# Moving residuals and block sums to GpSimd, the per-row constant to ScalarE, and reordering VectorE's first work in a two-layer graph kernel

## The chip, the core and the metric

The kernel runs on one core of a Trainium2 chip, in one launch. The metric is the device time of that launch in microseconds (us): a median of 1521.02 us over three runs, which lie between 1520.96 and 1525.21 us. One more execution was recorded by the hardware profiler. It took 1521.21 us, and the span from its first to its last instruction was 1519.2 us. All times with decimals below are from that execution, counted from the start of its span.

Five engines work side by side, each on a queue of its own: TensorE (PE in the profile; its weight loads are the row PEld), VectorE (DVE), ScalarE (ACT), GpSimd (POOL) and SyncE (SP, which here only issues DMAs).

## What is computed

The input x has 128 batches b, each of 128 rows (nodes) and 512 columns. The matrix adj is 128x128 and sparse. Cut to what matters:

```python
h = relu(layernorm(x))                        # over the 512 columns
A = einsum('od,bdn->bon', adj, h); C = A + b0 # layer 0: both weights are adj
x = x + max_over_last(relu(A[:, :, None, :] + (C - A)[:, :, :, None]))
h = relu(layernorm(x))                        # layer 1
q, k, v = h @ Wq + bq, h @ Wk + bk, h @ Wv + bv
w = softmax(q @ k.T / 8 + (adj == 0) * -1e9)  # 8 heads of 64
x = x + w @ v
```

Since C - A is the bias b0 of the row, layer 0 adds one number per row and batch, c = relu(max of A over the columns + b0). A constant added to a row doesn't change its layernorm, so both layers use the same h. The output is thus x + c + attention(h), and the bias of v can be added to x.

## The kernel before

**Groups.** Four batches make a group; there are 32 groups, g = 0 to 31, with b = 4g the first batch of group g and m = b + 8 the first batch of the group two further on. The kernel is software-pipelined over groups: while group g is attended to, q and k of group g+1 are computed, and the norms of group g+2.

**Products.** The projections h·W are 512x512 by 512x(4·128), done with seven block products in place of eight (p1, p6, p2, p7, p5, p4, p3), on sums and differences of the blocks of W and of h. p4 and p3 of most groups are split once more in the same way into 128x128 blocks (p43a and p43b). These need:
- sums of W: `weight_sums` (L381) and, one level down, `weight_blocks` (L369), made once per weight;
- sums of h: `h_sum` (L345, four per group) and, one level down, `h_blocks` (L354 to L356, two calls of three instructions per group), which fill the tile h2, of which there is one buffer.

TensorE multiplies (`mm` L418, `block_mm` L484); VectorE and ScalarE take results out of PSUM (L433, L439, L457, L466, L487). In `p43b`, TensorE writes a scratch bank, VectorE adds it to the tile u (L487, in `more`), and TensorE's last four matmuls of p43b write the same scratch bank again.

**Norms.** `norm(m)` makes statistics on VectorE (L279 to L282) and, on GpSimd, the reciprocal deviation and its product with the mean (L284, L286). `norm_end(m)` applies them on ScalarE (L289) and then adds the bias of v to x on GpSimd (L295, `add_bv`). `blocks(m)` transposes h in 32x32 blocks on VectorE (L302) and `move` sends two batches of them with 16 DMAs on SP's queue to their places in the tile hT (L312). `adjacency(m)` multiplies h by adj on TensorE (L327) and takes the maximum on VectorE (L328); every fourth one makes c (L330).

**Attention.** `scores` (L567, exponentials on ScalarE L575), `mask` (L579, eight per group, on GpSimd except at the end), `apply` (L597; VectorE divides by the sums, L614 and L615), and `residual` (L625): out = x + c + o in one VectorE instruction per batch, followed by the DMA to out (L629). In the last group, two of the four go to ScalarE and GpSimd (L627, L628).

**The order is written out by hand.** Within `tc.manual_schedule()` each engine executes its instructions in the order in which the program emits them. A group is `apply` of the group before, `scores`, and then 18 steps (six in the last group, which has v alone), most of them one product; a table `todo` says what is emitted after the product of each step:

```python
part += [[p.p1], [p.p6], [p.p2]]                       # v, then q and k of g+1
...
    part += [[p.p7, p.p43a], [p.p5], [p.p43b]]         # steps 3, 4, 5 for v
...
for s, ps_ in enumerate(part):
    for p in ps_:
        p()
    for f, *args in todo[s]:
        f(*args)
```

So work given to step 4 stands, on its engine, behind what p5 of v emits and ahead of what p43b of v emits. Group 0, the last but one (group 30) and the last one have tables that differ in places. The beginning, ahead of the loop, is a straight list (L655 to L697): norms of group 0, transposes and q of group 0 by plain products (`plain_q`), sums of Wk and of h, norms of group 1, and then the seven products of k of group 0.

Of the kernel before, what the change touches and what calls it, by code (L numbers as in the profile page):

```python
# [47 lines left out]
AF = mybir.ActivationFunctionType  # L48
ALU = mybir.AluOpType
# [4 lines left out]
G = 4  # L54
# [113 lines left out]
def tile_adj_preln_d2(  # L168
# [13 lines left out]
    nc = tc.nc  # L182
    B, D, N = x.shape
    NG = B // G
# [22 lines left out]
    def fast(ctx):  # L207
# [8 lines left out]
        CNT, w_of, O = [], {}, {}  # L216
        X, HN, TB, HT, HB, H2, QT, KT, C, AMAX, WA, RSTD, NMR, PR = ({} for _ in range(14))
# [5 lines left out]
        def x_of(b):  # L223
            return X[b // 2][:, b % 2, :]
# [63 lines left out]
        def norm_end(m):  # L288
            nc.scalar.activation(HN[m], x_of(m), AF.Relu, scale=RSTD[m], bias=NMR[m])  # L289
            if m >= G:  # L290
                add_bv(m)
# [32 lines left out]
        def adjacency(m):  # L324
            g, i = divmod(m, G)
            pa = bank(7 if g > 0 else 5 + i % 2)
            nc.tensor.matmul(pa, adjT, HN[m], start=True, stop=True)  # L327
            nc.vector.reduce_max(AMAX[g][:, i : i + 1], pa, axis=AX.X)  # L328
            if i == G - 1:
                nc.vector.tensor_scalar(C[g], AMAX[g], b0_sb, 0.0, op0=ALU.add, op1=ALU.max)  # L330
# [9 lines left out]
        def h_sum(g, k):  # L340

            o, a, b = ("t1 b12 b11", "t2 b22 t1", "t3 b22 b12", "t4 b21 t2")[k].split()
            if k == 0:
                h_quarters(g)
            nc.vector.tensor_sub(HB[g][o], HB[g][a], HB[g][b])  # L345

        def h_blocks(g, k):

            if k == 0:
                H2[g] = one.tile([P, 2, 4, D], F32, name="h2")  # L350
            b = HB[g]["b22 t4".split()[k]].rearrange("p t c d -> p c t d")
            t = H2[g][:, 1 - k]

            nc.vector.tensor_sub(t[:, 0:2], b[:, :, 1], b[:, 0])  # L354
            nc.vector.tensor_sub(t[:, 2], b[:, 1, 1], t[:, 0])
            nc.vector.tensor_sub(t[:, 3], b[:, 1, 0], t[:, 2])  # L356

        def weight_blocks(eng, n):

# [29 lines left out]
        class Products:  # L389
# [48 lines left out]
            def add(self, out, bank, more):  # L438
                nc.vector.tensor_tensor(out, self.view(bank), self.view(more), op=ALU.add)  # L439
# [141 lines left out]
        def apply(g, n_last=G):  # L581
# [31 lines left out]
            for po, rs, oo in parts:  # L613
# [3 lines left out]
                    rs.unsqueeze(2).to_broadcast([P, rs.shape[1], HD]), op=ALU.mult,  # L617
                )

        def residual(b, eng=nc.vector):  # L620
            g, i = divmod(b, G)
            y = O[g][:, i]
            x_b, c_b = x_of(b), C[g][:, i : i + 1]
            if eng is nc.vector:
                eng.scalar_tensor_tensor(y, x_b, c_b, y, op0=ALU.add, op1=ALU.add)  # L625
            else:
                nc.scalar.activation(x_b, x_b, AF.Identity, bias=c_b)  # L627
                eng.tensor_tensor(y, x_b, y, op=ALU.add)  # L628
            nc.sync.dma_start(out[b], y)  # L629

        def count(b0, b1):
# [10 lines left out]
        def next_norms(m):  # L642

            return {
                0: [(norm_end, m), (norm, m + 1), (norm_end, m + 1)],
                7: [(adjacency, m)], 8: [(norm, m + 2), (norm_end, m + 2), (blocks, m)],
                9: [(blocks, m + 1), (move, m + 1)],
                12: [(norm, m + 3), (norm_end, m + 3), (adjacency, m + 1)],
                13: [(blocks, m + 2)],
                14: [(blocks, m + 3), (move, m + 3), (adjacency, m + 2)],  # L650
            }

        with tc.manual_schedule():

            for m in range(G):  # L655
                norm(m)
                if m < 2:
                    norm_end(m)
            transposes(0)
            transposes(1)  # L660
            norm_end(2)
            norm_end(3)
            nc.vector.tensor_single_scalar(live, adjT, 0.0, op=ALU.not_equal)
            adjacency(0)
            adjacency(1)
            transposes(2)
            transposes(3)
            weight_sums(nc.gpsimd, "v")
            plain_q(0, 0)
            adjacency(2)  # L670
            plain_q(0, 1)
            adjacency(3)
            weight_sums(nc.vector, "k")
            for k in range(4):
                h_sum(0, k)
            norm(G)
            norm_end(G)
            norm(G + 1)
            norm_end(G + 1)
            plain_q(1, 0)  # L680
            blocks(G)
            blocks(G + 1)
            move(G + 1)
            plain_q(1, 1)
            k = Products(0, "k")
            more = {
                0: [(adjacency, G), (norm, G + 2), (norm_end, G + 2)],
                1: [(norm, G + 3), (norm_end, G + 3), (blocks, G + 2)],
                2: [(adjacency, G + 1)], 3: [(blocks, G + 3), (move, G + 3)],
                4: [(adjacency, G + 2)], 5: [(adjacency, G + 3)],  # L690
            }
            for s, p in enumerate((k.p1, k.p6, k.p2, k.p7, k.p5, k.p4, k.p3)):
                p()
                for f, m in more.get(s, ()):
                    f(m)
            weight_sums(nc.gpsimd, "q")
            weight_blocks(nc.gpsimd, "q")  # L697
            for g in range(NG):
                b = g * G
                if g > 0:  # L700
                    apply(g - 1)
                scores(g)
                part = []
                for p in [Products(g, "v")] + [Products(g + 1, n) for n in "qk" if g + 1 < NG]:
                    part += [[p.p1], [p.p6], [p.p2]]
                    if p.n == "v" and g in (0, NG - 1):
                        part += [[p.p7], [p.p5], [p.p4, p.p3]]
                    else:
                        part += [[p.p7, p.p43a], [p.p5], [p.p43b]]
                todo = {s: [] for s in range(len(part))}  # L710

                def add(s, *what):
                    todo[s].append(what)

                m = b + 2 * G
                if g + 1 < NG:
                    if g > 0:
                        for i in range(G):
                            residual(b - G + i)
                    if m < B:  # L720
                        norm(m)
                    if 0 < g < NG - 1:
                        add(0, adjacency, m - 1)
                    for k, s in enumerate((1, 2, 2, 3) if g > 0 else (3, 3, 4, 5)):
                        add(s, h_sum, g + 1, k)
                    for k, s in enumerate((6, 7)):
                        add(s, h_blocks, g + 1, k)
                    if g + 2 < NG:
                        for s, l in next_norms(m).items():
                            for what in l:  # L730
                                add(s, *what)
                    else:
                        add(6, count, 0, b)
                    eng = nc.gpsimd if m < B else nc.vector
                    at = (8, 9, 9, 10, 10, 13, 14, 15) if m < B else (4, 8, 8, 12, 12, 13, 14, 14)
                    for k, s in enumerate(at):
                        add(s, mask, eng, b + k // 2, k % 2)
                    if g + 2 < NG:
                        add(0, load, 2 * g + 5)
                    if g + 3 < NG:  # L740
                        add(8, load, 2 * g + 6)
                else:
                    for k, s in enumerate((0, 0, 0, 0, 2, 2, 3, 4)):
                        add(s, mask, nc.vector, b + k // 2, k % 2)
                    for i, s in enumerate((0, 0, 0, 1)):
                        add(s, residual, b - G + i)
                if g == 0:
                    add(8, weight_blocks, nc.gpsimd, "k")
                    for i in range(G):
                        add(15, add_bv, i)  # L750
                    add(15, weight_blocks, nc.gpsimd, "v")
# [6 lines that stand above are left out]
            g = NG - 1  # L758
            apply(g, 2)
            count(B - 2 * G, B)  # L760
            for i in range(G):
                residual(g * G + i, nc.gpsimd if i < 2 else nc.vector)
            pc = bank(1)
            for k in range(2):
                nc.tensor.matmul(pc[0:1, 0:1], CNT[k], ones, start=k == 0, stop=k == 1)
            nc.scalar.copy(flag, pc[0:1, 0:1])
# [38 lines left out]
```

## Time and profile before

| | busy us | share of the span |
|---|---|---|
| TensorE matmuls (PE) | 1499.8 | 99% |
| TensorE weight loads (PEld) | 1323.4 | 87% |
| VectorE (DVE) | 1152.1 | 76% |
| GpSimd (POOL) | 597.3 | 39% |
| ScalarE (ACT) | 426.6 | 28% |

A matmul's row starts when the one ahead of it has been let go, not when it has ended: they are pipelined, so a row's length is more than its share of the engine. What a matmul costs TensorE is read from one start to the next. In the timeline a row "1.89 PE ... x8" is eight matmuls; the next row starts 1.73 us after it where nothing waits, 0.216 us for each. Likewise the 128x128 block products start 0.112 us apart, and an adjacency product (two instructions) takes 0.86 us. Groups 1 to 29 start 46.57 us after one another. The granted clock of TensorE is full in all stretches up to 1480 us.

### The profile page before, as it was taken

The numbers are of one execution on the slowest core, as the hardware profiler recorded it, in microseconds if no ns is written. First come the engines' busy times: TensorE is split into PE (matmuls) and PEld (weight loads), VectorE is DVE, ScalarE is ACT, GpSimd is POOL, SyncE is SP. The second block draws the span as 40 slices with busy tenths as digits, with TensorE's granted clock in tenths as the row PEclk, the third lists the DMA queues.
The fourth block names the chain that finished last, engine by engine and source line by source line (L and its number), as shares of the span: only waits on it lengthen the run. The fifth ranks groups of instructions, "written<-read, shape, count | busy, mean of one in ns | idle before, by whom it ended". The sixth has DMA issues, their size and how long they took to land.

```text
span 1519.2 us, 32776 instructions
## 1 busy us (share of the span) xinstructions
PE 1499.8 (99%) x12909; PEld 1323.4 (87%) x12909; DVE 1152.1 (76%) x2485; ACT 426.6 (28%) x844; POOL 597.3 (39%) x670
## 2 busy tenths in 40 slices
PE   7999999999999999999999999999999999999997
PEld 5888888888888888898888888888988888888887
DVE  5577777777787777777777877777777778777776
ACT  3223232222232232323322332323233222222221
POOL 4574443343432444423434324344234343243400
PEclk9999999999999999999999999999999999999999
DMA  4233122332222321223312223222233122232211
GB/s 165 54 83 84 27 74 73 81 84 47 58 74 75 84 70 40 74 73 82 85 29 75 73 77 84 59 49 74 73 84 84 28 74 73 78 84 41 53 35 57
DMA packets 307803, 105.28 MB, mean 69 GB/s; under 512 B 273152, under 2 KB 273280, under 8 KB 307648
## 3 DMA queue, kind: packets, MB, share of 16 engines
q1 hardware_dynamic: 307328, 102.84, 26.1%
q8 instruction: 103, 1.69, 0.5%
q14 instruction: 52, 0.43, 0.1%
q0 software_dynamic: 176, 0.27, 0.1%
q10 hardware_dynamic: 144, 0.07, 0.0%
HBM read 37.03 MB, written 33.55 MB: 46 GB/s over the span
## 4 chain that ended last, share of the span: by engine, by line
PE 96%; DVE 2%; POOL 1%; ACT 0%; issue 0%; DMA 0%; DVEq 0%; POOLq 0%; ACTq 0%
PE bk L418 54%; PE bk L484 19%; PE bk L597 8%; PE bk L567 8%; PE bk L327 7%; PE bk L543 0%; POOL w L579 0%; POOL ssk_sb L369 0%; PE bk L321 0%; DMA xp<-in_x_dram 0%; POOL rstd L284 0%; DVE sk_sb L381 0%; POOL xp L295 0%; DVE hs L345 0%; ACT hn L289 0%
## 5 line engine op out<-in xcount | busy, mean ns | idle before, releaser
L284 POOL TENSOR_TENSOR rstd<-ve,mhalf 128x1 f32<-128x1 f32 x128 | 71.0, 554 | 703.9 <-DVE ve L282 703.6
L487 DVE TENSOR_TENSOR u<-u,bk 128x256 f32<-128x256 f32 x552 | 206.4, 415 | 127.5 <-PE bk L484 123.2
L579 POOL TENSOR_TENSOR w<-w,live 128x512 f32<-128x512 f32 x240 | 297.6, 1274 | 0.0
L575 ACT ACTIVATE w<-bk 128x512 f32<-128x512 f32 x256 | 128.8, 625 | 363.5 <-PE bk L567 363.5
L295 POOL TENSOR_TENSOR xp<-xp,bv_sb 128x512 f32<-128x512 f32 x128 | 165.8, 1297 | 117.9 <-ACT hn L289 117.9
L418 PEld LDWEIGHTS bk<-hs,sk_sb 128*128 128x128 f32 x768 | 143.6, 190 | 44.7 <-issue 29.2
L418 PE MATMUL bk<-hs,sk_sb 128*128 128x256 f32 x768 | 181.3, 379 | 0.0
L418 PE MATMUL bk<-sv_sb,hs 128*128 128x256 f32 x768 | 181.2, 379 | 0.0
L418 PE MATMUL bk<-hs,sq_sb 128*128 128x256 f32 x744 | 175.9, 379 | 0.1
L418 PEld LDWEIGHTS bk<-sv_sb,hs 128*128 128x128 f32 x768 | 143.6, 190 | 31.1 <-issue 14.3
L418 PEld LDWEIGHTS bk<-hs,sq_sb 128*128 128x128 f32 x744 | 138.9, 190 | 18.1 <-DVE u L457 0.5
L289 ACT ACTIVATE hn<-xp,nmr,rstd 128x512 f32<-128x512 f32 x124 | 100.9, 814 | 169.1 <-POOL nmr L286 169.0
L328 DVE TENSOR_REDUCE amax<-bk 128x1 f32<-128x512 f32 x128 | 87.9, 686 | 56.4 <-PE bk L327 56.4
L327 PE MATMUL bk<-hn,adjT 128*128 128x512 f32 x248 | 126.7, 592 | 0.3 <-ACT hn L289 0.3
L597 PE MATMUL bk<-v,w 128*64 128x65 f32 x4096 | 126.5, 222 | 0.0
L597 PEld LDWEIGHTS bk<-v,w 128*64 128x64 f32 x4096 | 122.1, 137 | 4.1 <-issue 0.3
L418 PE MATMUL bk<-hT,wk_sb 128*128 128x256 f32 x512 | 121.2, 380 | 3.1 <-ACT u L433 3.1
L418 PE MATMUL bk<-wv_sb,hT 128*128 128x256 f32 x512 | 124.3, 386 | 0.0
L567 PE MATMUL bk<-qT,kT 64*128 64x128 f32 x2048 | 122.9, 275 | 0.0
L567 PEld LDWEIGHTS bk<-qT,kT 64*128 64x128 f32 x2048 | 116.8, 188 | 2.5 <-issue 0.3
L418 PE MATMUL bk<-hT,wq_sb 128*128 128x256 f32 x496 | 117.3, 379 | 0.0
L466 DVE TENSOR_TENSOR u<-bk,u 128x512 f32<-128x512 f32 x95 | 65.7, 691 | 64.3 <-PE bk L418 64.3
(151 smaller groups left out, 2355.2 us busy)
## 6 DMA issues: line engine op xcount, KB each, us to landing
out_dram<-o SPq DMA_DIRECT2D x128, 256.0 KB, 2.4
xp<-in_x_dram SPq DMA_DIRECT2D x62, 512.0 KB, 4.9
hT<-tb SPq DMA_DIRECT2D x992, 32.0 KB, 1.9
xp<-in_x_dram SPq DMA_DIRECT2D x4, 256.0 KB, 3.8
wq_sb<-in_L_gnn_Wq_dram SPq DMA_DIRECT2D x2, 512.0 KB, 7.2
wk_sb<-in_L_gnn_Wk_dram SPq DMA_DIRECT2D x2, 512.0 KB, 9.1
wv_sb<-in_L_gnn_Wv_dram SPq DMA_DIRECT2D x2, 512.0 KB, 10.4
bv_sb<-in_L_gnn_bv_dram POOLq DMA_DIRECT2D x1, 256.0 KB, 6.5
```

The costliest lines, as they stand in the source:

```text
L284: nc.gpsimd.tensor_tensor(rstd, ve, mhalf, op=ALU.pow)
L289: nc.scalar.activation(HN[m], x_of(m), AF.Relu, scale=RSTD[m], bias=NMR[m])
L295: nc.gpsimd.tensor_tensor(x_m, x_m, bv_sb, op=ALU.add)
L327: nc.tensor.matmul(pa, adjT, HN[m], start=True, stop=True)
L328: nc.vector.reduce_max(AMAX[g][:, i : i + 1], pa, axis=AX.X)
L418: nc.tensor.matmul(bank[:, r, :], lhs, rhs, start=first and r == 0 and c == 0, stop=r == 1 and c == 1, skip_group_check=True,)
L484: nc.tensor.matmul(out, lhs, rhs, start=start, stop=True, skip_group_check=True)
L487: nc.vector.tensor_tensor(to, to, what, op=ALU.add)
L567: nc.tensor.matmul(psc[j][:, f, :], KT[g][r, f, i * D : (i + 1) * D], QT[g][r, f, i * D : (i + 1) * D], start=True, stop=True,)
L575: nc.scalar.activation(w[:, j], psc[j], AF.Exp, scale=HD ** -0.5)
L579: eng.tensor_tensor(w[:, j], w[:, j], live_h, op=ALU.mult)
L597: nc.tensor.matmul(pav[r, c : c + HE], w[:, h % 2, h // 2, r], V[:, i, h, :], start=True, stop=True,)
```

## The change

1. **`h_blocks` on GpSimd.** The six differences per group (L354 to L356) become GpSimd instructions, emitted after steps 5 and 6 where they were after 6 and 7.
2. **`residual` in two parts.** A new `add_c` adds c to x in place on ScalarE, after steps 2, 5, 9 and 15 of the group (after steps 1 to 4 in the last group). `residual` is then o = x + o, on GpSimd for the groups 1 to 30, on VectorE in the last group's steps; at the very end two are on GpSimd and two on VectorE as before.
3. **Norms and transposes of group g+2.** `norm(m + 1)` is emitted with `norm(m)` ahead of step 0. `blocks(m)` goes from step 8 to step 4, `blocks(m + 1)` and the DMAs of `move(m + 1)` from step 9 to step 6. The other two batches stay where they were.
4. **`h_sum`** of groups from 1 on goes from steps 1, 2, 2, 3 to 0, 1, 2, 2.
5. **Beginning.** The sums of Wk and of h and the norms of batches 4 and 5 are emitted ahead of the maxima of batches 2 and 3, where they stood after them. TensorE's own order stays as it was; on ScalarE the two norm_end stand between the outputs of `plain_q`.
6. **`weight_blocks` of Wk** in group 0: on VectorE ahead of step 0, where it was on GpSimd after step 8.

```diff
@@ h_blocks
-            nc.vector.tensor_sub(t[:, 0:2], b[:, :, 1], b[:, 0])
-            nc.vector.tensor_sub(t[:, 2], b[:, 1, 1], t[:, 0])
-            nc.vector.tensor_sub(t[:, 3], b[:, 1, 0], t[:, 2])
+            for o, x, y in (
+                (t[:, 0:2], b[:, :, 1], b[:, 0]),
+                (t[:, 2], b[:, 1, 1], t[:, 0]),
+                (t[:, 3], b[:, 1, 0], t[:, 2]),
+            ):
+                nc.gpsimd.tensor_tensor(o, x, y, op=ALU.subtract)
...
+        def add_c(b):
+            x_b = x_of(b)
+            nc.scalar.activation(x_b, x_b, AF.Identity, bias=C[b // G][:, b % G : b % G + 1])
+
         def residual(b, eng=nc.vector):
-            g, i = divmod(b, G)
-            y = O[g][:, i]
-            x_b, c_b = x_of(b), C[g][:, i : i + 1]
-            if eng is nc.vector:
-                eng.scalar_tensor_tensor(y, x_b, c_b, y, op0=ALU.add, op1=ALU.add)
-            else:
-                nc.scalar.activation(x_b, x_b, AF.Identity, bias=c_b)
-                eng.tensor_tensor(y, x_b, y, op=ALU.add)
+            y = O[b // G][:, b % G]
+            eng.tensor_tensor(y, x_of(b), y, op=ALU.add)
             nc.sync.dma_start(out[b], y)
@@ next_norms
-                0: [(norm_end, m), (norm, m + 1), (norm_end, m + 1)],
-                7: [(adjacency, m)], 8: [(norm, m + 2), (norm_end, m + 2), (blocks, m)],
-                9: [(blocks, m + 1), (move, m + 1)],
+                0: [(norm_end, m), (norm_end, m + 1)],
+                4: [(blocks, m)], 6: [(blocks, m + 1), (move, m + 1)], 7: [(adjacency, m)],
+                8: [(norm, m + 2), (norm_end, m + 2)],
@@ the beginning
             plain_q(0, 0)
-            adjacency(2)
-            plain_q(0, 1)
-            adjacency(3)
             weight_sums(nc.vector, "k")
             for k in range(4):
                 h_sum(0, k)
+            adjacency(2)
             norm(G)
             norm_end(G)
+            plain_q(0, 1)
             norm(G + 1)
             norm_end(G + 1)
+            adjacency(3)
             plain_q(1, 0)
@@ the loop over groups
-                            residual(b - G + i)
+                            residual(b - G + i, nc.gpsimd)
                     if m < B:
                         norm(m)
+                        norm(m + 1)
...
-                    for k, s in enumerate((1, 2, 2, 3) if g > 0 else (3, 3, 4, 5)):
+                    for k, s in enumerate((0, 1, 2, 2) if g > 0 else (3, 3, 4, 5)):
                         add(s, h_sum, g + 1, k)
-                    for k, s in enumerate((6, 7)):
+                    for k, s in enumerate((5, 6)):
                         add(s, h_blocks, g + 1, k)
...
+                for i in range(G):
+                    add((2, 5, 9, 15)[i] if g + 1 < NG else i + 1, add_c, b + i)
                 if g == 0:
-                    add(8, weight_blocks, nc.gpsimd, "k")
+                    weight_blocks(nc.vector, "k")
```

## The prediction

> **What bounds the kernel now.** I read the page's first part first, then TensorE's own waits, then the timeline wherever TensorE's starts are further apart than its matmuls need.
>
> ```profile
> PE 1499.8 (99%) x12909; PEld 1323.4 (87%) x12909; DVE 1152.1 (76%) x2485; ACT 426.6 (28%) x844; POOL 597.3 (39%) x670
> ```
>
> ```profile
> PE bk L418 <- ACT u L433: 3.1, 1, 3.1
> ...
> PE bk L484 <- DVE u L487: 0.8, 1, 0.8
> ```
>
> TensorE is busy for 99% and waits visibly almost nowhere, so work taken off VectorE in the middle of the kernel can gain nothing. Start-to-start distances agree: in groups 1 to 29, 46.57 us each, no start is late by more than 0.15 us, and those are the same places in every group (the switches to and from scores). What can be won are single stalls. The first is in the beginning:
>
> ```profile
> 29.25 0.81 ACT L289 ACTIVATE hn<-xp,nmr,rstd 128x512 f32<-128x512 f32 x1 [8.06 <-POOL nmr L286]
> 30.11 1.12 PE L327 MATMUL bk<-hn,adjT 128*128 128x512 f32 x2 [0.32 <-ACT hn L289]
> 31.08 1.89 PE L418 MATMUL bk<-hs,sk_sb 128*128 128x256 f32 x8
> 32.32 0.81 ACT L289 ACTIVATE hn<-xp,nmr,rstd 128x512 f32<-128x512 f32 x1 [2.26 <-POOL nmr L286]
> 33.04 1.56 ACT L550 ACTIVATE qT<-bk,bq_sb 128x256 f32<-128x256 f32 x4
> 34.47 0.86 ACT L433 ACTIVATE p1a<-bk,bk_sb 128x256 f32<-128x256 f32 x2
> 35.18 0.87 ACT L433 ACTIVATE u<-bk,bk_sb 128x256 f32<-128x256 f32 x2
> 36.11 1.99 PE L418 MATMUL bk<-hT,wk_sb 128*128 128x256 f32 x8 [3.14 <-ACT u L433]
> ```
>
> ScalarE's queue is blocked by norm_end of batch 5 until 32.32; behind it stand the outputs of plain_q and of p1, and p2 of k may not overwrite p1's bank until 36.11. The second, in group 0, is the 0.8 us at 88.32. The lines that decide the sign come last, VectorE and TensorE at the end of v's p5 and p43b, first in a middle group, then in group 30:
>
> ```profile
> 667.86 0.69 DVE L439 TENSOR_TENSOR v<-bk,u 128x512 f32<-128x512 f32 x1
> ...
> 668.46 0.41 DVE L487 TENSOR_TENSOR u<-u,bk 128x256 f32<-128x256 f32 x1
> ...
> 669.44 0.61 PE L484 MATMUL bk<-ssv_sb,h 128*128 128x128 f32 x4
> ```
>
> ```profile
> 1459.55 0.69 DVE L439 TENSOR_TENSOR v<-bk,u 128x512 f32<-128x512 f32 x1
> ...
> 1460.16 0.68 DVE L579 TENSOR_TENSOR w<-w,live 128x512 f32<-128x512 f32 x1
> ...
> 1460.76 0.41 DVE L487 TENSOR_TENSOR u<-u,bk 128x256 f32<-128x256 f32 x1
> ...
> 1460.91 0.39 PE L484 MATMUL bk<-sv_sb,h 128*128 128x128 f32 x2
> ...
> 1461.22 0.71 PE L484 MATMUL bk<-ssv_sb,h 128*128 128x128 f32 x4
> 1461.77 1.89 PE L418 MATMUL bk<-hT,wq_sb 128*128 128x256 f32 x8
> ```
>
> The last four matmuls of p43b overwrite the scratch bank that L487 reads. In the middle group L487 follows p5's add at once and they start on time. In group 30 a mask, given to step 4, stands between: L487 starts 1.21 us after p5's add instead of 0.60, the four matmuls start at 1461.22 where 1460.91 + 2 x 0.112 = 1461.13 was due, and then need 0.55 us instead of 0.45. Together 0.19 us. No list of waits shows it: TensorE's rows overlap it.
>
> **The Trainium skill.** "Perfetto Trace Analysis", section "Identifying the Most-Contended Engine", says that matmul busy time is no measure of how close TensorE is to its limit, because matmuls are pipelined. The trace agrees: it counts group 30's 0.19 us as busy. "GPSIMD Engine Reference", section "Key points", says that GpSimd shares its SBUF interfaces with VectorE, with contention when VectorE runs instructions with two SBUF inputs. The trace agrees: near 97 us GpSimd's 128x128 differences take 0.91 us beside L625 and 0.46 us elsewhere, and L625 starts are 0.86 apart instead of 0.66. The same section calls VectorE about twice as fast for elementwise work; here 128x512 with two SBUF inputs starts each 0.60 us on VectorE and each 1.23 us on GpSimd.
>
> **The change part by part.**
>
> *Beginning.* The stall is 0.47 (adjacency due 27.91 + 1.73 = 29.64, starts 30.11) + 0.11 + 3.30 (p2 due 31.08 + 1.73) + 0.10 for restarting = **3.98 us**. After the change VectorE has the sums as soon as Wk is there (landing 13.2 at the latest: issued 3.60, 9.6 us): 8 x 0.60, until 18.1; then the maximum of batch 2, then norm of batch 4 until 20.0. GpSimd is in the sums of Wv from 16.50 until 21.4, so it sets the norm: L284 and L286 take 0.95, norm_end(4) on ScalarE ends at 23.2, L295 ends at 24.5, the norm of 5 at 25.5, norm_end(5) at 26.3. The plain_q outputs follow, the last one when TensorE ends it (28.1 to 28.9), then p1's from 29.84 to 31.4. p2 is due at 29.64 + 0.86 + 1.73 = 32.23: no stall. The reordered maxima keep nobody waiting, since their banks aren't used again until later. Contention of VectorE's sums with the sums of Wv between 16.5 and 18.1 could delay GpSimd by up to 1.8 us; there is 2.6 us of room. Move of 4 and 5 is issued 6 us earlier, on an idle SP queue. Taken: -4.0; bounds -4.0 and -1.8 (all four sums of Wv twice as long).
>
> *weight_blocks of Wk on VectorE.* 8 instructions of 0.21 to 0.33 us: 1.7 to 2.6 us, ahead of group 0's v, while scores run for 3.8 us and VectorE has an idle gap of 4.21 us. Nothing. It takes 3.6 us from GpSimd between the masks; so L284 of batch 11, which waited until 83.40, is made about 4 us earlier relative to TensorE, even with h_blocks. The 0.98 us (88.32 against 85.61 + 1.73) + 0.10 restart go: **-1.1**.
>
> *h_blocks on GpSimd.* No 128x256 row there; between 0.42 (128x128) and 1.23 (128x512) start to start, I take 0.73. Two calls: 3.1 us, at most 4.1. They wait for the end of v's p43b (669.9, one h2 buffer), with GpSimd idle in the middle group from 665.7 to 677.0, and end by 674.2; q's p43a reads h2 first at 678.1. Behind them stands only the norm of m+2, due 677. Nothing. In group 30 VectorE loses 0.95 us ahead of the count, which made p7 late by 0.30 + 0.10: **-0.4**.
>
> *add_c.* L627 shows two in 1.33 us, so 2.7 us per group on ScalarE, behind outputs of steps 2, 5, 9 and 15, each with over 1 us until ScalarE's next use. Nothing.
>
> *Residuals on GpSimd.* L628: 1.23 us each, from 655.4 (end of apply's last L615) to 660.3. Queued behind are the two norms: L284 and L286 of m end 661.2, norm_end(m) 662.0, that of m+1 663.0, earlier than today's 664.2, since norm(m+1) no longer waits for L295. On SP the outs come 2 us later, and behind them one load, used at step 8, some 9 us after landing. VectorE saves 2.7 us that nobody waits for. Nothing; at the end two instructions of 0.60 replace 0.66: **-0.1**.
>
> *h_sum one step earlier.* hT must have landed: the 16 + 16 move DMAs (0.69 us each) now start earlier, with the second load queued between them (landing 12 us ahead of its norm). Nothing.
>
> *blocks(m) at step 4.* L302 stands on VectorE between p5's add and L487 of v's p43b, the place of group 30's mask. To what follows, a mask takes 0.60 us and L302 0.63 (85.20 to 85.83). So the four matmuls are late by 0.09 + 0.03 + 0.10 = **0.22 us**, in groups 1 to 29 (29 of them): **+6.4**. Bounds 0.19 and 0.25: 5.5 and 7.3. blocks(m+1), at step 6, lies where h_blocks was. Nothing.
>
> Sum: -4.0 - 1.1 - 0.4 - 0.1 + 6.4 = +0.8 us on the span of 1519.2. Other executions lie 1.8 us over that span (1521.02), and so does its own time (1521.21): **1521.8 us**, with the bounds 1520.9 to 1524.9.
>
> **Rivals.** About 0.3%, or 4.6 us, is what a measurement of this kernel can tell from no change.
> - *The stall at p43b doesn't come*: then the gains stand alone, -5.6: 1515.4. For it: TensorE's room for L487 is 0.5 us, so a small shift of p5's add would do. Against it: group 30. Chance 0.22.
> - *Contention, slower*: GpSimd's residuals and sums with two SBUF inputs run late and lie beside VectorE's chain p5's add, L302, L487. Price: +0.20 us per group (L625's 0.86 against 0.66), 29 x 0.42 - 5.6 = +6.6: 1527.6. It decides from +0.13 per group. Against it: GpSimd should be idle from 664.5 to 669.9, and none of the three has two SBUF inputs. Chance 0.16.
> - *The beginning gains nothing*, because GpSimd's norm of batch 5 comes over 2.6 us late and ScalarE's queue still blocks p1's outputs: +4.0, 1525.8. Against it: the landing of Wk. Chance 0.04.
> - The forecast: 0.58.
>
> Range: forecast and first rival hold 0.80, and with the last one the range is 1515.0 to 1526.0; the likeliest case alone has 1520.9 to 1524.9. Faster by over 0.3%: 0.22; within: 0.58; slower: 0.20.
>
> **What would show it.** Beginning: p2 of k directly behind p6, scores of group 0 at 43.5 instead of 47.52. Group 0: no wait for L487. Middle: groups 46.8 us apart instead of 46.57, the late start always in the last four matmuls of v's p43b, with L302 ahead of L487. GpSimd at some 55%, h_blocks ended 4 us ahead of q's p43a. Wrong it would be if groups stay at 46.57 (first rival) or pass 46.92, or if a wait for GpSimd appears on TensorE or VectorE.

## The result, and the profile after

| | before | after |
|---|---|---|
| median of the runs, us | 1520.99 (1520.95 to 1525.21) | 1539.40 (1539.03 to 1540.25) |
| span of the profiled execution, us | 1519.17 | 1538.42 |

The ratio is 1.0115, 95% interval 1.0097 to 1.0133: **slower**, by about 1.2%. That is 17.6 us above the forecast of 1521.8 and far outside its range. After the change `block_mm` is L487, `more` L490, p5's add L442, p6's L460, p7's L469, `h_blocks` L359 and `residual` L630; the lines up to L345 kept their numbers.

The first part of the page, busy times:

```profile
PE 1507.3 (98%) x12909; PEld 1322.5 (86%) x12909; DVE 1080.2 (70%) x2187; ACT 507.0 (33%) x970; POOL 869.5 (57%) x968
```

VectorE lost 72 us of work, GpSimd took 272 us more, and neither is near full. TensorE still looks busy for 98%. The waits of TensorE (line that waited, what it waited for, us in total, times, longest) say where to look:

```profile
PE bk L487 <- DVE u L490: 15.6, 29, 0.7
```

Before, that wait came once in the whole kernel (0.8 us). Now it comes 29 times, which is groups 1 to 29. Start-to-start distances turn this into an account:

| us | beginning | group 0 | groups 1 to 29, each | group 30 |
|---|---|---|---|---|
| before | 35.14 | 47.12 | 46.563 | 44.99 |
| after | 31.15 | 46.03 | 47.367 | 44.58 |
| difference | -3.99 | -1.09 | +0.804 | -0.41 |
| predicted | -3.98 | -1.1 | +0.22 | -0.4 |

("Beginning" runs from the first plain_q matmul to the start of group 0's scores; each number under "each" is a median.) The single stalls went just as predicted. The middle costs 29 x 0.804 = 23.3 us instead of 6.4, and that is the error, nearly all of it. Together the stretches give +17.8 us, while the span grew by 19.25. The rest lies ahead of the first plain_q matmul (at 12.38 us before, 13.29 after) and behind the start of the last group (29.09, 29.52); over all the profiles below, these two vary from 11.7 to 13.3 and from 27.4 to 29.5 us.

The timeline of the beginning, after:

```profile
28.24 0.81 ACT L289 ACTIVATE hn<-xp,nmr,rstd 128x512 f32<-128x512 f32 x1 [1.53 <-POOL nmr L286]
...
28.96 1.55 ACT L553 ACTIVATE qT<-bk,bq_sb 128x256 f32<-128x256 f32 x4
...
30.75 0.84 ACT L436 ACTIVATE p1a<-bk,bk_sb 128x256 f32<-128x256 f32 x2 [0.24 <-PE bk L421]
31.41 1.89 PE L421 MATMUL bk<-hs,sk_sb 128*128 128x256 f32 x8
31.48 0.84 ACT L436 ACTIVATE u<-bk,bk_sb 128x256 f32<-128x256 f32 x2
...
33.13 1.89 PE L421 MATMUL bk<-hT,wk_sb 128*128 128x256 f32 x8
```

norm_end of batch 5 is done at 29.05, the outputs of plain_q and of p1 follow (p1's even wait 0.24 us for TensorE), and p2 starts at 31.41 + 1.72: the stall of 3.3 us is gone.

The timeline of a middle group, after, from the residuals to the end of v's p43b:

```profile
660.98 4.95 POOL L630 TENSOR_TENSOR o<-xp,o 128x512 f32<-128x512 f32 x4 [9.29 <-DVE o L618]
...
668.09 3.39 POOL L295 TENSOR_TENSOR xp<-xp,bv_sb 128x512 f32<-128x512 f32 x2
...
668.59 1.75 DVE L345 TENSOR_TENSOR hs<-hT 128x512 f32<-128x512 f32 x1
...
670.27 1.76 DVE L345 TENSOR_TENSOR hs<-hT,hs 128x512 f32<-128x512 f32 x1
...
671.44 1.89 PE L421 MATMUL bk<-sv_sb,hs 128*128 128x256 f32 x8
...
671.95 0.68 DVE L469 TENSOR_TENSOR u<-bk,u 128x512 f32<-128x512 f32 x1
672.73 1.08 DVE L490 TENSOR_TENSOR u<-u,bk 128x256 f32<-128x256 f32 x3
...
673.87 0.71 PE L487 MATMUL bk<-ssv_sb,h 128*128 128x128 f32 x4 [0.53 <-DVE u L490]
...
675.76 0.61 PE L487 MATMUL bk<-ssv_sb,h 128*128 128x128 f32 x4
```

And the same two kinds of rows in the timeline of before (the group there starts about 5.5 us earlier):

```profile
661.10 1.27 POOL L295 TENSOR_TENSOR xp<-xp,bv_sb 128x512 f32<-128x512 f32 x1 [0.93 <-ACT hn L289]
...
662.61 0.68 DVE L345 TENSOR_TENSOR hs<-hT 128x512 f32<-128x512 f32 x1
663.33 0.69 DVE L345 TENSOR_TENSOR hs<-hT,hs 128x512 f32<-128x512 f32 x1
...
664.36 1.39 POOL L295 TENSOR_TENSOR xp<-xp,bv_sb 128x512 f32<-128x512 f32 x1 [0.93 <-ACT hn L289]
...
665.24 0.69 DVE L466 TENSOR_TENSOR u<-bk,u 128x512 f32<-128x512 f32 x1 [0.62 <-PE bk L418]
```

Read the second column. h_sum (L345), the same instruction, takes 0.68 us in before and 1.75 us in after where it begins while GpSimd is in L295; L295 itself goes from 1.27 to 1.70 each (3.39 for two). In before the two L295 leave a hole of almost 2 us, and h_sum fills it. In after they run back to back, 668.09 to 671.48, right over h_sum's last two. Behind those, VectorE does p7's add at 671.95; it used to wait 0.62 us for TensorE there, now it comes late. Three L490 follow, and p43b's first four matmuls, which overwrite the bank that L490 reads, start at 673.87. Due was 671.44 + 1.73 = 673.17: 0.70 late, and a first matmul after a wait lets the next one start 0.10 later than usual. The sum is the group's 0.80.

The forecast's own stall, at the *last* four matmuls of p43b, isn't there: they start at 675.76, which is 673.87 + 1.79 + 0.10, so nothing but the restart is added. The larger stall gave L490 the time.

### The profile page after: what moved, and what is told of

It is laid out like the page before. It is cut to its first block, busy times and chain, and to the rows that moved or that the text cites. A ratio compares the mean times of both kernels' runs of the same rounds, so it can differ in the third digit from the quotient of the medians.

```text
span 1538.4 us, 33066 instructions
## 1 busy us (share of the span) xinstructions
PE 1507.3 (98%) x12909; PEld 1322.5 (86%) x12909; DVE 1080.2 (70%) x2187; ACT 507.0 (33%) x970; POOL 869.5 (57%) x968
## 5 line engine op out<-in xcount | busy, mean ns | idle before, releaser
L630 POOL TENSOR_TENSOR o<-xp,o 128x512 f32<-128x512 f32 x122 | 151.0, 1270 | 312.6 <-DVE o L618 269.3
L490 DVE TENSOR_TENSOR u<-u,bk 128x256 f32<-128x256 f32 x552 | 206.0, 415 | 120.3 <-PE bk L487 113.1
L295 POOL TENSOR_TENSOR xp<-xp,bv_sb 128x512 f32<-128x512 f32 x128 | 186.1, 1464 | 61.0 <-ACT hn L289 61.0
L421 PEld LDWEIGHTS bk<-hs,sq_sb 128*128 128x128 f32 x744 | 139.1, 190 | 17.5
L284 POOL TENSOR_TENSOR rstd<-ve,mhalf 128x1 f32<-128x1 f32 x128 | 83.5, 653 | 95.1 <-DVE ve L282 94.9
L469 DVE TENSOR_TENSOR u<-bk,u 128x512 f32<-128x512 f32 x95 | 65.3, 688 | 91.8 <-PE bk L421 89.7
```

The lines of the kernel that those rows point to most:

```text
L284: nc.gpsimd.tensor_tensor(rstd, ve, mhalf, op=ALU.pow)
L295: nc.gpsimd.tensor_tensor(x_m, x_m, bv_sb, op=ALU.add)
L421: nc.tensor.matmul(bank[:, r, :], lhs, rhs, start=first and r == 0 and c == 0, stop=r == 1 and c == 1, skip_group_check=True,)
L490: nc.vector.tensor_tensor(to, to, what, op=ALU.add)
L630: eng.tensor_tensor(y, x_of(b), y, op=ALU.add)
```

## Experiments

**C**, the theory: VectorE's h_sum (two inputs in SBUF) is slowed by a GpSimd instruction beside it; the change puts the two add_bv on top of it. Rivals: **S**, it's h_sum's earlier place in VectorE's order; **R**, it's the residuals on GpSimd as such, whatever else is moved; and blocks(m) at step 4, the forecast's cause. Each ratio below is against runs of before on the same chip, taken together with it. Their median is 1523.3 to 1523.8 us there, not 1521.0; the last section says why. The middle, the median distance of groups 1 to 29, doesn't depend on that.

### add_bv out of h_sum's way, blocks(m) a step later, and both

`bv_late` (from after) lets both add_bv wait until step 6 (False keeps norm_end from calling add_bv); `blocks5` moves blocks(m) only; `bv_late_blocks5` does both.

```diff
-                0: [(norm_end, m), (norm_end, m + 1)],
-                4: [(blocks, m)], 6: [(blocks, m + 1), (move, m + 1)], 7: [(adjacency, m)],
+                0: [(norm_end, m, False), (norm_end, m + 1, False)],
+                4: [(blocks, m)], 6: [(blocks, m + 1), (move, m + 1), (add_bv, m), (add_bv, m + 1)], 7: [(adjacency, m)],
```

```diff
-                4: [(blocks, m)],
+                5: [(blocks, m)],
```

> The changed kernel with one edit: the two additions of v's bias to x (add_bv of m and m+1, GpSimd) are emitted behind h_blocks in step 6, so that they can't run beside VectorE's four h_sum. Theory C (contention of h_sum with add_bv makes v's p43b late by 0.80 us in 29 groups): h_sum takes 0.68 us again, the 0.80 us are gone, the recorded 0.22 us per group behind blocks(m) at step 4 comes out instead: 1539.4 - 23.2 + 6.4 = 1522.6 us. Theory B (the place of blocks(m) alone makes the stall): unchanged, 1539. Rival R (GpSimd's queue is simply late because of the four residuals, and something waits for it): 1539 or more, since this edit makes GpSimd's work later still.

> The changed kernel with blocks(m) emitted after step 5 instead of step 4, nothing else. Theory C: TensorE is already late at the start of p43b, so the last four matmuls of p43b lose nothing to L302 now: 1539 us, within 1 us of the changed kernel. Theory B (as recorded in the prediction, 0.22 us in each of 29 groups): 1533.0 us; if blocks(m) makes the whole 0.80 us: 1516.

> Both edits together. Theory C with the recorded step for blocks(m): no stall is left in the middle groups, 46.57 us each, 1522.6 - 6.4 = 1516.2 us, faster than the kernel before by 4.8 us. If blocks(m) at step 4 costs nothing, this equals bv_late. If contention isn't the cause: 1533 or more.

| | us | ratio, 95% | middle |
|---|---|---|---|
| bv_late | 1521.25 | 0.9988, 0.9981 to 0.9995 | 46.750 |
| blocks5 | 1538.97 | 1.0102, 1.0085 to 1.0119 | 47.373 |
| bv_late_blocks5 | 1515.93 | 0.9952, 0.9936 to 0.9969 | 46.563 |

All three times came within 1.4 us of what C expected. The timeline of `bv_late`:

```profile
660.02 0.68 DVE L345 TENSOR_TENSOR hs<-hT 128x512 f32<-128x512 f32 x1
...
660.62 0.68 DVE L345 TENSOR_TENSOR hs<-hT,hs 128x512 f32<-128x512 f32 x1
...
662.18 0.69 DVE L469 TENSOR_TENSOR u<-bk,u 128x512 f32<-128x512 f32 x1 [0.88 <-PE bk L421]
...
665.40 0.70 DVE L302 STREAM_TRANSPOSE tb<-hn 128x512 f32<-128x512 f32 x1
...
666.03 0.38 DVE L490 TENSOR_TENSOR u<-u,bk 128x256 f32<-128x256 f32 x1
666.16 0.39 PE L487 MATMUL bk<-sv_sb,h 128*128 128x128 f32 x2
666.46 0.71 PE L487 MATMUL bk<-ssv_sb,h 128*128 128x128 f32 x4
```

h_sum is back at 0.68 and p7's add waits for TensorE again. What is left is the forecast's stall, in its place: L302 stands ahead of L490, and the last four start at 666.46 where 666.16 + 0.22 was due. The median group shows its full price, 46.750 - 46.563 = **0.187 us**, 5.4 us over 29 groups. `blocks5` adds the other half: while the contention is there, moving blocks(m) is worth nothing. With both gone, the middle is before's to the nanosecond.

### The residuals alone, in the kernel before

`residual_alone` is before with the new `add_c` and `residual`, all else as it was.

```diff
-                            residual(b - G + i)
+                            residual(b - G + i, nc.gpsimd)
...
+                for i in range(G):
+                    add((2, 5, 9, 15)[i] if g + 1 < NG else i + 1, add_c, b + i)
```

> The kernel before with the residual part alone (c added by ScalarE, the addition of o on GpSimd); h_sum, norms and h_blocks stay where they were. Theory C: one add_bv meets the first h_sum, which costs about 1.1 us of VectorE's room ahead of p7's add and leaves no or little delay (up to 0.1 us per group); the norms of m and m+1 stay apart: 1521 to 1524 us. Rival R (the residuals on GpSimd are the cost by themselves): 1535 to 1540 us.

1527.01 us, ratio 1.0025 (1.0017 to 1.0034), middle 46.710: +0.147. R is refuted as an account of the 0.80, but C's estimate of no cost is missed as well. The residuals push the norms back on GpSimd, so the two add_bv, still apart here, come later and lie beside the first h_sum (1.48 us) and the fourth (1.03 us). The fourth stands ahead of p5's add; a block product is 0.04 us late behind it, and the restart adds 0.10.

### Is it the earlier place of h_sum?

`hsum_old_steps` (from after) puts h_sum back.

```diff
-                    for k, s in enumerate((0, 1, 2, 2) if g > 0 else (3, 3, 4, 5)):
+                    for k, s in enumerate((1, 2, 2, 3) if g > 0 else (3, 3, 4, 5)):
```

> The changed kernel with h_sum back at steps 1, 2, 2, 3; all else as changed. Theory C (the clash comes from add_bv of m and m+1 lying back to back behind the residuals, at the time of h_sum): three h_sum still lie beside them: 1537 to 1541 us. Theory S (the step earlier of h_sum made the clash): 1521 to 1524 us.

1544.25 us, ratio 1.0136 (1.0119 to 1.0153), middle 47.513. S is refuted: the old place is worse still. The first two h_sum take 1.57 and 1.65 us beside add_bv, and the last one again stands ahead of p5's add. Three places in the group are then late, by 0.61, 0.09 and 0.25 us together with their restarts. C's range was missed, since it had only one stall in it.

### How much of it is GpSimd's second input?

`bv_one_input` (from after) replaces add_bv's instruction by one with a single tensor input, at the same place. It leaves out the bias of v.

```diff
-            nc.gpsimd.tensor_tensor(x_m, x_m, bv_sb, op=ALU.add)
+            nc.gpsimd.tensor_scalar(x_m, x_m, 0.0, 1.0, op0=ALU.add, op1=ALU.mult)
```

> The changed kernel with add_bv on GpSimd made an instruction with one tensor input (x times 1 plus 0, in place) at the same place in the queue: the bias of v is left out (it is zero in the inputs). Theory C1 (VectorE's h_sum is slowed only where GpSimd too reads two tensors): h_sum takes 0.68 us again and the stall at p43b goes, as in bv_late: 1521.3 us. Theory C2 (any GpSimd instruction on SBUF slows VectorE's two-input instructions): h_sum stays at 1.2 us or more beside it and most of the 0.80 us stay: 1532 to 1539 us.

1521.1 us, ratio 0.9985 (0.9978 to 0.9992), middle 46.750: the time of `bv_late`. The timeline:

```profile
660.17 2.07 POOL L295 TENSOR_SCALAR xp<-xp 128x512 f32<-128x512 f32 x2
...
660.67 1.09 DVE L345 TENSOR_TENSOR hs<-hT 128x512 f32<-128x512 f32 x1
...
661.68 1.09 DVE L345 TENSOR_TENSOR hs<-hT,hs 128x512 f32<-128x512 f32 x1
...
662.82 0.69 DVE L469 TENSOR_TENSOR u<-bk,u 128x512 f32<-128x512 f32 x1
```

The time alone would say "no contention with one input", and it would be wrong: h_sum takes 1.09 us, between 0.68 and 1.75. Neither theory had that. So the contention isn't confined to two inputs on GpSimd, and the ends of the rows show what sets its size. Here the second h_sum ends at 662.77, 0.53 us after GpSimd's second instruction (662.24). In `after` it ended at 672.03, 0.55 us after GpSimd's (671.48). It is so everywhere: of the 410 h_sum in all these traces that began beside a GpSimd instruction with two inputs (128x256 or 128x512), with at least 0.19 us of it still to go, 409 ended 0.54 to 0.56 us after its end (one began together with it and went first), and the 58 of `bv_one_input` 0.54 us after it. This reads as a wait for GpSimd's instruction to end, not as a slower rate. With one input that instruction is shorter (1.04 us in place of 1.70), so the wait is; nothing here shows a further effect of the second input. p7's add then comes early enough: the room ahead of it decides whether TensorE sees the wait.

### Moving add_bv in other ways

`norm_apart` (from after) puts norm(m + 1) back between the two norm_end; `residual_on_vector` gives the residuals of the groups back to VectorE.

```diff
-                0: [(norm_end, m), (norm_end, m + 1)],
+                0: [(norm_end, m), (norm, m + 1), (norm_end, m + 1)],
...
-                        norm(m + 1)
```

```diff
-                            residual(b - G + i, nc.gpsimd)
+                            residual(b - G + i)
```

> The changed kernel with norm(m+1) back in step 0, behind norm_end(m), so that add_bv(m) and add_bv(m+1) lie about 2 us apart and h_sum meets one of them at a time. Theory C: about half of the clash: 0.3 to 0.6 us per group over 46.56 instead of 0.80: 1525 to 1533 us. If the two add_bv don't have to be neighbours for it: 1539.

> The changed kernel with the four residuals back on VectorE (x + o, with c added by ScalarE as changed). GpSimd's norms come about 1.3 us earlier, VectorE's norms 2.4 us later. Theory C: add_bv of m and m+1 now meet h_sum 0 and 1 in place of 1, 2 and 3, so p6's add is late (p7 waits some 0.3 to 0.5 us) and the 0.19 us behind blocks(m) come back: 1528 to 1534 us. If the residuals on GpSimd are the whole cause: 1521 to 1523.

| | us | ratio, 95% | middle | mean h_sum, ns |
|---|---|---|---|---|
| norm_apart | 1531.65 | 1.0053, 1.0036 to 1.0069 | 47.076 | 715 |
| residual_on_vector | 1528.20 | 1.0028, 1.0018 to 1.0038 | 46.990 | 1024 |

(before 687, after 1193.) Both times lie in the expected ranges, but `norm_apart` for another reason than the one given: its h_sum is hardly slowed at all. Its 0.51 us per group are blocks(m)'s 0.19 and a wait of v's p7 for p6's add, which now stands on VectorE behind the first h_sum as well as the statistics of m + 1; before, only the statistics stood there (0.22 us, and 0.10 for the restart). A right number didn't prove the reason. In `residual_on_vector` the norms come earlier, the back-to-back add_bv fall on h_sum 0 and 1 (1.63 and 1.16 us), and p7 starts 0.13 + 0.10 us late behind p6's add; with blocks(m)'s 0.19 that is its +0.43. So pairing the norms brings add_bv back to back by itself, and the residuals on GpSimd decide which h_sum they hit.

### The beginning alone

`beginning_alone` is before with the new beginning (part 5 of the change) and Wk's weight_blocks on VectorE.

```diff
-            adjacency(2)
-            plain_q(0, 1)
-            adjacency(3)
             weight_sums(nc.vector, "k")
             for k in range(4):
                 h_sum(0, k)
+            adjacency(2)
...
-                    add(8, weight_blocks, nc.gpsimd, "k")
+                    weight_blocks(nc.vector, "k")
```

> The kernel before with the new beginning alone (sums of Wk and h and norms ahead of the maxima) and weight_blocks of Wk on VectorE in group 0; the middle is that of before, 46.56 us per group. By the recorded steps: -4.0 for the beginning and -1.1 for group 0, so 5.1 us under the kernel before: about 1516 us. If the stalls only move elsewhere: 1521.

1516.77 us (1516.05 to 1516.88), ratio 0.9955 (0.9938 to 0.9971); span 1514.12, which is 5.05 less than before, where -3.99 and -1.09 were worked out from after. Its own beginning takes 31.25 us, its group 0 46.03, and its middle is 46.563. `bv_late_blocks5`, with all of the change's other parts, has a span of 1514.20; in the account by stretches, group 30's 0.4 us is all that those other parts gain.

### The contention put into the kernel before

`clash_in_before` repeats two masks on GpSimd between the two norms of the kernel before, beside h_sum; live is 0 or 1, so a mask repeated changes no value. `masks_elsewhere` is its control: two repeated masks at the end of step 15.

```diff
-                0: [(norm_end, m), (norm, m + 1), (norm_end, m + 1)],
+                0: [
+                    (norm_end, m), (mask, nc.gpsimd, m - 2 * G, 0), (mask, nc.gpsimd, m - 2 * G, 1),
+                    (norm, m + 1), (norm_end, m + 1),
+                ],
```

```diff
+                        for k in range(2):
+                            add(15, mask, nc.gpsimd, b + 3, k)
```

> The kernel before, with nothing of the change in it, and two of GpSimd's mask multiplications made once more in step 0 of each group (the mask is 0 or 1, so the result stays) between add_bv(m) and the norm of m+1, at the time of VectorE's first h_sum. Theory C: h_sum 0 and 1 take up to 1.75 us, p7's add comes about 1.2 us late, TensorE waits 0.8 to 1.0 us at v's p43b in 30 groups: 1544 to 1551 us. If the slow h_sum in the changed kernel has another cause than GpSimd's two-tensor instruction beside it: 1521 to 1523 us.

> Control: the kernel before with two masks made once more at the end of step 15 (batch b+3), where VectorE has only instructions with one tensor in SBUF. The same 2.5 us more on GpSimd per group. Theory C: no cost, 1521 to 1522 us. If more work on GpSimd costs by itself: 1540 or more.

`clash_in_before` took 1561.76 us, ratio 1.0242 (1.0225 to 1.0259), middle 47.883; `masks_elsewhere` 1524.47 us, ratio 1.0002 (0.9994 to 1.0011), middle 46.563, not moved at all. The timeline of `clash_in_before`:

```profile
680.76 2.94 POOL L579 TENSOR_TENSOR w<-w,live 128x512 f32<-128x512 f32 x2
681.05 1.52 DVE L345 TENSOR_TENSOR hs<-hT 128x512 f32<-128x512 f32 x1
682.61 1.64 DVE L345 TENSOR_TENSOR hs<-hT,hs 128x512 f32<-128x512 f32 x1
...
686.56 1.21 DVE L345 TENSOR_TENSOR hs<-hT,hs 128x512 f32<-128x512 f32 x1
...
686.70 0.71 PE L484 MATMUL bk<-ssv_sb,h 128*128 128x128 f32 x4 [0.44 <-DVE u L487]
...
688.42 0.49 PE L484 MATMUL bk<-sv_sb,hT 128*128 128x128 f32 x2 [0.35 <-DVE v L439]
```

The same amount of GpSimd work costs nothing in one place and 1.32 us per group in another, and h_sum's duration shows why: 1.52 and 1.64 us, with a line of GpSimd that isn't add_bv. The size was under-estimated. The first stall lies where after's does (0.71 us with its restart). The masks also delay the second add_bv onto the fourth h_sum, which holds up p5's add: a second stall of 0.61.

## Why the prediction was wrong

- *Beginning*, -4.0: right (-3.99). The contention it named there occurred: three of the four sums of h took 1.65 to 1.75 us beside the sums of Wv (17.5 to 22.5 us). So norm_end of batch 5 ended 1.8 us later than forecast, counted from the first plain_q matmul. That stayed within the room of 2.6 us.
- *weight_blocks*, -1.1, and *h_blocks in group 30*, -0.4: right (-1.09 and -0.41).
- *h_blocks*, *add_c*, and *residuals* as plain work: nothing. `bv_late_blocks5` has all of them and before's middle of 46.563. h_blocks ended 4.0 us ahead of q's p43a, as said.
- *blocks(m) at step 4*, +0.22 per group: right mechanism and place, mis-sized a little: 0.187, just under its lower bound of 0.19. In after itself it is covered by the larger stall.
- **The step that failed** is "Residuals on GpSimd ... Nothing". It followed GpSimd's queue up to norm_end(m) at 662.0 and norm_end(m+1) at 663.0 and stopped there. Counted from the end of `apply`, both times were right within 0.5 us. But each norm_end is followed by an L295, and two norm_end one microsecond apart mean two L295 of 1.27 us back to back, from 662.0 on, in the stretch where VectorE has h_sum. "h_sum one step earlier ... Nothing" has the same gap: it looked only at when h_sum's data land, not at what runs beside it. But the earlier place did no harm by itself, since `hsum_old_steps` is slower still (47.513). In the place of the zero, `bv_late` shows 47.367 - 46.750 = 0.62 us per group, 17.9 us over 29, against a miss of 17.6.
- *Rival "Contention, slower"*: the right mechanism in the wrong place and at the wrong price. It looked for an overlap with p5's add, L302 and L487, none of which has two inputs in SBUF, and took +0.20 us from L625. The instruction hit was h_sum, +1.07 us each. The L625 near 97 us were no price for it: each of the four ended 0.55 us after the GpSimd instruction beside it, as h_sum does, and that one is a short one (128x128). The Trainium skill, "GPSIMD Engine Reference", section "Key points", names the condition the prediction had quoted, two SBUF inputs on VectorE; h_sum meets it.

## What to carry to other kernels

Where instructions are moved between VectorE and GpSimd, list every two-input VectorE instruction of the stretch and follow GpSimd's queue to its *last* instruction there, not to the one that someone waits for. Price an overlap by how long the other engine's instruction still has to run, not by what a shorter pair lost elsewhere in the trace. Then compare an instruction's duration before and after: a mean that rises from 0.69 to 1.19 us for unchanged work points straight at h_sum, where the list of TensorE's waits names only the add that comes after it (L490).

## What the runs showed of the hardware

- **The contention is a wait, in both directions.** VectorE's 128x512 sum of two SBUF tensors takes 0.68 us alone, up to 1.77 us beside GpSimd's 128x512 sum of two tensors and 1.09 us beside GpSimd's 128x512 instruction with one. In each case it ends 0.54 to 0.56 us after the GpSimd instruction that had begun first. The other way round, where GpSimd's 128x512 instruction with two inputs begins while an h_sum runs, it ends 1.12 to 1.14 us after that h_sum (325 cases), and the one-input instruction 0.48 us after it (56 cases); so GpSimd's sum goes from 1.27 up to 1.70 us. VectorE's instructions with one SBUF input didn't change beside GpSimd's sums: in `after`, bn_stats takes 0.684 us both beside them (60 that overlap by at least 80%) and away from them (39), and the adds of a PSUM tile to an SBUF tile take 0.69 (L442) and 0.42 us (L490) in both places. Whether reading or writing makes the wait wasn't tried.
- **A stall of 3.3 us can halve the clock after it.** Before's runs spread from 1520.8 to 1525.2 us, and the longer ones list a lower mean clock (0.996 at 1524.9 us, 0.998 at 1520.9); kernels with the new beginning keep within 1.6 us. Four profiled kernels have before's beginning and its stall. Two of them, `masks_elsewhere` and `clash_in_before`, show a clock of 0.50 behind it; `before` and `residual_alone` don't, nor, in these windows, does any kernel without the stall. The windows of `masks_elsewhere` (window, length, busy us of PE, PEld, DVE, ACT and POOL, granted clock, DMA share, GB/s):

```profile
34.00:36.00 2.00, 0.00 (x0) 0.00 (x0) 1.86 (x6) 2.00 (x7) 0.87 (x2) 0.89 0.10 16
36.00:38.00 2.00, 1.56 (x4) 1.29 (x5) 1.68 (x5) 1.20 (x3) 0.97 (x3) 0.50 0.29 49
38.00:40.00 2.00, 2.00 (x6) 1.57 (x5) 0.44 (x1) 0.05 (x1) 1.82 (x3) 0.50 0.29 49
40.00:42.00 2.00, 2.00 (x4) 0.95 (x3) 0.04 (x1) 1.49 (x3) 1.15 (x1) 0.50 0.29 49
```

  The same window in before's profile:

```profile
36.00:38.00 2.00, 1.89 (x9) 1.69 (x10) 1.68 (x5) 0.87 (x2) 0.97 (x3) 1.00 0.31 52
```

  TensorE idles through 34 to 36 in both; then it has 0.50 of its clock for 6 us in the one, and matmuls start 0.427 us apart instead of 0.216; in the other nothing happens. The beginning took 38.06 instead of 35.14 us. The Trainium skill, "TensorE: Matmul & The Clock Gate", Part 1, describes a throttle to half rate after an idle window of that order, with a window that runs freely; 0.50 in two of the four profiles and 1.00 in the other two agree with that. The new beginning, with group 0's share of 1.09 us, is therefore worth 5.05 us against an undisturbed execution, and 6.6 us against the median of 1523.3 of the before runs beside it.
